# Attention, projection and block transform on one core: x of four projection tiles loaded in the last head, and five output buffers

## The chip, the core and the metric

The kernel runs on one core of a Trainium2 chip. A core has a matrix engine (TensorE, "PE" in the profile, its weight loads "PEld"), VectorE ("DVE"), ScalarE ("ACT"), GpSimd ("POOL"), the synchronisation engine ("SP"), which in this kernel only issues transfers, and 16 DMA engines that all queues share. The on-chip memory is called SBUF, the memory of the matrix results PSUM. The metric is the device time of one execution in microseconds; less is better. A time is the median of several runs. The profile is of one further execution.

## The reference

x has the shape (1, 48, 256, 256) in float32. Two layers follow each other, each with a group normalisation and a residual:

```python
x = x + L0(gn(x))     # attention over 4x4 patches, 8 heads
x = x + L1(gn(x))     # three matrices over w, h and c in 64x64 windows
```

```python
def L0(x, w_qkv, w_dw, temperature, w_proj):
    qkv = jnp.einsum('bchw,oc->bohw', x, w_qkv)
    qkv = dwconv3x3(qkv, w_dw)
    q, k, v = heads(unfold(split(qkv)))          # 8 heads, 96 x 4096 (and a border)
    q, k = l2norm(q), l2norm(k)
    attn = softmax(einsum('bhcn,bhcm->bhnm', q, k) * temperature)
    out = fold(einsum('bhcn,bhnm->bhcm', v, attn))
    return einsum('bchw,oc->bohw', out, w_proj)

def L1(x, Ws, Hs, Cs):
    xb = x.reshape(B, C, H // 64, 64, W // 64, 64)
    return einsum('bcphqw,twW,thH,tcC->bCpHqW', xb, Ws, Hs, Cs).reshape(B, C, H, W)
```

The functions are shortened; "..." of shapes and padding is left out.

## The kernel before, in words

**Stages.** First x is read once for its statistics, the pointwise part of two heads is computed and head 0 is convolved (`depthwise_first`). Then the eight heads run, in a block whose instructions keep the order in which they are written (`tc.manual_schedule()`). Then comes the projection with the first residual and the statistics of the second layer (lines 726 to 788), and at last the second layer in 64 x 64 windows (from line 791).

**A head.** A head has 16 groups (`NG`) of two blocks of 128 rows. For each block `scores` (L337, L566) multiplies 128 queries with all 4096 keys and takes exponentials into a tile `e` of 16 KB a partition; there are three such tiles. `weigh` (L595, L606) then multiplies the exponentials of both blocks with the values and adds to four accumulators `oacc`, one for each k of `NK` = 4. While a head runs, the convolution of the next head is done beside it by `Depthwise`, and the next head's keys and values are loaded. In the last head (`more` is false) there is none of that. `load_query(h, g + 2)` is issued on SP in group g, into one of two buffers.

**Keys.** Head h has eight key tiles of 4 KB a partition, `keys[h, m]`, in 14 buffers taken in turn. Tile m of head h is number 8h + m, so the last head's eight tiles fall in places 0 to 7 of the ring.

**Outputs.** In the last group of a head, `store(h, m)` for m = 0 to 7 transposes a piece of the accumulators (L612), copies it from PSUM into `oo` (L614, ScalarE, two buffers of 2 KB) and issues two transfers of 96 KB from the POOL queue to the buffer `os_` in device memory (L616). Outputs 0 and 1 come after k = 1, 2 and 3 after k = 2, 4 and 5 after k = 3, 6 and 7 at the end.

**Projection.** It has 8 tiles (t) of 16 rows in each half of the picture; both halves lie side by side in 96 partitions. For each tile and half SP loads `pot` (the outputs, L740) and `pxt` (x, L741), 48 x 16 KB = 768 KB each, into pools of three buffers. Tile 0 needs outputs 0 and 4, tiles 2t and 2t+1 need outputs t and t+4. TensorE projects in four steps (L746), VectorE adds x in place (L753) and takes statistics (L757), and POOL issues the store of the sum (L762) to `x1s`. The x load of tile t + 3 goes into the buffer that tile t's store reads. This part has no written order: it is ordered at build time by readiness and by place in the program. Each engine then carries out its own list strictly in order, SP and POOL as queues of transfers.

**Memory.** Pools lie behind one another from the low end of a partition. Before the change, behind the constants: `cv` (the convolution's buffers, 52 KB), `ahead` (queries, 14 key tiles, values), `ae` (three tiles e), `asm` (small tiles and `oo`) and `ao`; the partition is full. A later pool that takes the place of earlier ones waits, with its first instruction, until all tiles of the pools under it have been read for the last time. The pool `pj` (48 KB for pot, 48 KB for pxt) lies over `cv` and `ahead`.

Of the kernel before, what the change touches and what calls it, by code (L numbers as in the profile page):

```python
# [8 lines left out]
F32 = mybir.dt.float32  # L9
F32R = mybir.dt.float32r  # L10
# [6 lines left out]
C = 48  # L17
H = W = 256
HALF = H // 2
P2 = 2 * C  # L20
KS = 4
KK = KS * KS
NH = 8
HD = C * KK // NH
# [9 lines left out]
PX = W // KS  # L34
# [5 lines left out]
TP = 256  # L40
# [5 lines left out]
def conv_preact_kernel(  # L46
# [15 lines left out]
    nc = tc.nc  # L62
    xc = x.rearrange("b c y x -> (b c) y x")
# [34 lines left out]
    for s in range(2):  # L98
        r = slice(s * C, (s + 1) * C)
        for h in range(NH if s == 0 else H0):  # L100
            o = s * M0 + h * HC if h < H0 else (h - H0) * HC
            nc.gpsimd.dma_start(
                out=(wq[r] if h < H0 else wr[0:C])[:, o : o + HC].rearrange("c (z e) -> c z e", z=3),
                in_=w_qkvT.rearrange("c (z h e) -> h c z e", z=3, h=NH)[h],
# [198 lines left out]
    NM = NT // 512  # L303
# [99 lines left out]
    with tc.tile_pool(name="xn", bufs=1) as xnp, tc.tile_pool(name="cst", bufs=1) as cst, tc.tile_pool(  # L403
        name="nps", bufs=2, space=PSUM
# [9 lines left out]
        for i, LR in enumerate(parts):  # L414
            j = sum(parts[:i])
            for s in range(2):
                eng = nc.sync if s == 0 else nc.scalar
                eng.dma_start(
                    out=xr[s * C : (s + 1) * C, j : j + LR, :], in_=xc[:, s * HALF + j : s * HALF + j + LR, :]
# [8 lines left out]
        for g, (w, k) in enumerate(((wq, P2), (wr, C))):  # L428
            m = w.shape[1]
# [48 lines left out]
                nc.sync.dma_start(out=rows, in_=ot[s * M0 : (s + 1) * M0])  # L478

    attention = ExitStack()  # L480
    cv = attention.enter_context(tc.tile_pool(name="cv", bufs=1))
    one = attention.enter_context(tc.tile_pool(name="one", bufs=2, space=PSUM))

    ots = [cv.tile([M1, 4, W + 2], F32, name=f"ot{i}") for i in range(NOT)]
# [5 lines left out]
    with tc.If(nc.values_load(large) > 0):  # L490
# [8 lines left out]
        with tc.tile_pool(name="mk", bufs=NM) as mk, tc.tile_pool(name="mq", bufs=2) as mq, tc.tile_pool(  # L499
            name="mps", bufs=2, space=PSUM  # L500
        ) as mps:
            for h in range(NH):
                kts = []
                for m in range(NM):
                    kt = mk.tile([128, 2, 512], F32R, name="mkt")
# [18 lines left out]
    with tc.tile_pool(name="ahead", bufs=2) as ah, tc.tile_pool(name="ae", bufs=3) as ae, tc.tile_pool(  # L524
        name="asm", bufs=6
    ) as asm, tc.tile_pool(name="ao", bufs=1) as ao, tc.tile_pool(name="big", bufs=3, space=PSUM) as big:
        MB = 8
        NK = NB // MB
        NG = NB // G
        keys, queries, values, oaccs = {}, {}, {}, {}  # L530

        def load_key(h, m, eng=nc.sync):
            keys[h, m] = ah.tile([128, 2, 512], F32R, name="kt", bufs=14)
            load_keys(keys[h, m], h, m, eng)

        def load_query(h, g):
# [71 lines left out]
        def store(h, m):  # L608

            pt = one.tile([HD, 4, 128], F32, name="pt", tag="one")  # L610
            for i in range(4):
                nc.tensor.transpose(pt[:, i, :], oaccs[h, m // 2][:, m % 2, i * HD : (i + 1) * HD], ident)  # L612
            oo = asm.tile([HD, 512], F32, name="oo", bufs=2)
            nc.scalar.copy(oo, pt.rearrange("p i n -> p (i n)"))  # L614
            for i in range(512 // TP):
                nc.gpsimd.dma_start(  # L616
                    out=os_[m * (512 // TP) + i, h * HD : (h + 1) * HD, :], in_=oo[:, i * TP : (i + 1) * TP]
                )
# [16 lines left out]
        with tc.manual_schedule():  # L635
            load_query(0, 1)
            block = scores(0, 0)
            for h in range(NH):
                more = h + 1 < NH
                rows = {r: Depthwise(h + 1, r) for r in range(CR + 1)} if more else {}  # L640
                for g in range(NG):
                    p, d, n = rows.get(g - 2), rows.get(g - 1), rows.get(g)

                    if h == 0 and 0 < g <= 6:
                        load_value(0, g + 1)
                    if more and CR + 2 <= g < CR + 6:
                        for m in range(2):
                            load_value(h + 1, (g - CR - 2) * 2 + m)
                    if more and CR + 3 <= g < CR + 6:
                        for m in range(2):  # L650
                            load_key(h + 1, (g - CR - 3) * 2 + m)

                    blocks = [normalised(*block)]
                    if p:
                        p.norm()
                        p.root()
                    block = scores(h, g * G + 1)
                    if more and g == NG - 1:
                        load_key(h + 1, 6)
                        load_key(h + 1, 7, nc.gpsimd)  # L660
                    if g + 2 < NG:
                        load_query(h, g + 2)
                    elif more:
                        load_query(h + 1, g + 2 - NG)
                    if p:
                        p.scale()
                    if d:
                        for t in range(1, 4):
                            d.tap(t)
                    second = block  # L670
                    if g + 1 < NG:
                        block = scores(h, (g + 1) * G)
                    elif more:
                        block = scores(h + 1, 0)
                    blocks.append(normalised(*second))
                    if d:
                        for t in range(4, 9):
                            d.tap(t)

                    if g == 0 and rows:  # L680
                        rows[0].load()

                    if h == 0 and 0 < g <= 6:
                        turn(0, g + 1)
                    if more and CR + 2 <= g < CR + 6:
                        for m in range(2):
                            turn(h + 1, (g - CR - 2) * 2 + m)
                    if g == 0 and h > 0:
                        for m in range(6, 8):
                            store(h - 1, m)  # L690
                    if p:
                        p.patches()
                        p.store((2,))
                        p.high()
                    if d:
                        d.square()
                    if n:
                        n.first()
                    for k in range(NK):
                        s = (h * NG + g) * NK + k  # L700
                        weigh(h, g, blocks, k)
                        if k == 0 and d:
                            d.reduce()
                        if k == 0 and p:
                            p.low(nc.gpsimd)
                            p.store((0, 1))
                        if s % 2:
                            for w in strips[s - 1] + strips[s]:
                                w.run(big.tile([128, 2, 512], F32, name="big"))
                            for w in strips[s + 1] + strips[s + 2]:  # L710
                                w.load()
                        elif s:
                            for w in strips[s - 2] + strips[s - 1]:
                                w.store()
                        if k == 2 and g + 1 in rows:
                            rows[g + 1].load()

                        if g == NG - 1 and k > 0:
                            for m in range(2 * k - 2, 2 * k):
                                store(h, m)  # L720
            for m in range(6, 8):
                store(NH - 1, m)
# [1 line left out]


    l1c = ctx.enter_context(tc.tile_pool(name="l1c", bufs=1))
    RP = TP // PX * KS
    NP = TP
    with tc.tile_pool(name="pj", bufs=3) as pj, tc.tile_pool(name="pjs", bufs=1) as pjs, tc.tile_pool(
        name="pps", bufs=3, space=PSUM  # L730
# [2 lines left out]
        ov = os_.rearrange("t (c k) n -> t c k n", k=KK)  # L733
        for t in range(HALF // RP):
            ot = pj.tile([P2, KK, NP], F32, name="pot")
            xt = pj.tile([P2, RP, W], F32, name="pxt")
            for s in range(2):
                r = slice(s * C, (s + 1) * C)
                y0 = s * HALF + t * RP
                nc.sync.dma_start(out=ot[r], in_=ov[s * (NT // 2 // TP) + t])  # L740
                nc.sync.dma_start(out=xt[r], in_=xc[:, y0 : y0 + RP, :])  # L741
            xv = xt.rearrange("p (py ki) (px kj) -> p ki kj py px", ki=KS, kj=KS)
            for ki in range(KS):
                ps = pps.tile([P2, KS, NP], F32, name="pps")
                for i in range(0, KS, 2):
                    nc.tensor.matmul(  # L746
                        ps[:, i : i + 2, :],
                        lhsT=wp,
                        rhs=ot[:, ki * KS + i : ki * KS + i + 2, :],
                        start=True,  # L750
                        stop=True,
                    )
                nc.vector.tensor_add(  # L753
                    xv[:, ki], ps.rearrange("p k (py px) -> p k py px", py=RP // KS), xv[:, ki]
                )
            for i in range(0, RP, 2):
                nc.vector.bn_stats(  # L757
                    st1[:, (t * RP + i) // 2, :], xt[:, i : i + 2, :].rearrange("p a b -> p (a b)")
                )
            for s in range(2):  # L760
                y0 = s * HALF + t * RP
                nc.gpsimd.dma_start(out=x1s[:, y0 : y0 + RP, :], in_=xt[s * C : (s + 1) * C])  # L762
# [23 lines left out]
        nc.tensor.matmul(pb1, lhsT=mrow, rhs=csn[0:C], start=True, stop=True)  # L786
        cbias = l1c.tile([128, T3 * C], F32, name="cbias")
        nc.vector.tensor_copy(cbias, pb1)


    with tc.tile_pool(name="lx", bufs=3) as lx, tc.tile_pool(name="lz", bufs=2) as lz, tc.tile_pool(
# [173 lines left out]
```

## Time and profile before

| what | us |
|---|---|
| time, median of 3 runs (3700.89 to 3706.79) | 3703.03 |
| the profiled execution | 3698.24 |
| its span, to which the profile's shares refer | 3696.2 |
| last head, first scores to last weighing | 2849 to 3222.85 |
| last output store issued | 3238.5 |
| first x load and first output load of the projection issued | 3210.05 and 3221.21 |
| first and last matmul group of the projection | 3238.89 and 3362.70 |
| last statistics of the projection done | 3379.9 |
| first load of the second layer issued | 3384.66 |

| engine | busy us | share of the span |
|---|---|---|
| PE | 3466.8 | 94% |
| PEld | 2905.8 | 79% |
| DVE | 2139.4 | 58% |
| ACT | 1873.3 | 51% |
| POOL | 542.9 | 15% |

How to read the profile: times are us from the span's start. "L746" is line 746 of the kernel. A group is written as line, engine, operation, output <- input. "Idle before" tells how long an engine had stood still and what ended that. The granted clock is the share of its full clock that TensorE was given. The DMA share is the mean busy share of the 16 DMA engines. The chain of waits goes back from the last instruction: at each step to what released it.

### The profile page before, as it was taken

Reading aid. Unit: us, or ns where it says so; the run is one execution under the profiler, and the core shown is the slowest. Engines: PE = TensorE matmul, PEld = TensorE weight load, DVE = VectorE, ACT = ScalarE, POOL = GpSimd, SP = SyncE. Lnnn points to the kernel's source line nnn. Section 1 sums busy time; section 2 is a strip of 40 time slices with the busy share of each in tenths; the row PEclk is TensorE's granted clock in tenths of the full one; section 3 lists DMA queues with packets and bytes.
Section 4 is the critical chain, followed back from the end, with each engine's and each line's share of the span. In section 5 each row is a group of like instructions: output and inputs, shape, how many; then the busy total and the mean of one; then the engine's idle time right before and its main releaser. Section 6 shows DMA issues by size and latency. Waiting matters only on the chain.

```text
span 3696.2 us, 100318 instructions
## 1 busy us (share of the span) xinstructions
PE 3466.8 (94%) x44252; PEld 2905.8 (79%) x44252; DVE 2139.4 (58%) x3514; ACT 1873.3 (51%) x2747; POOL 542.9 (15%) x628
## 2 busy tenths in 40 slices
PE   2869999999999999999999999999999999855998
PEld 1337777898888898988888989888889888713776
DVE  5454774189628953894399349925982222266654
ACT  0235676566546654665566556655664444300332
POOL 2030111012111211121122112201220000000011
PEclk9989999999999999999999999999999999966999
DMA  7455666533323332333233323332333100299774
GB/s 160 152 133 153 176 170 171 149 96 95 94 79 82 93 89 75 83 90 96 73 92 86 87 73 93 86 87 84 94 79 87 36 19 19 51 248 197 127 138 92
DMA packets 274146, 386.48 MB, mean 105 GB/s; under 512 B 77010, under 2 KB 211522, under 8 KB 269480
## 3 DMA queue, kind: packets, MB, share of 16 engines
q1 hardware_dynamic: 234790, 264.95, 27.4%
q0 software_dynamic: 35424, 106.40, 12.4%
q10 hardware_dynamic: 3490, 8.64, 1.1%
q8 instruction: 350, 5.73, 0.7%
q14 instruction: 92, 0.75, 0.1%
HBM read 234.76 MB, written 144.90 MB: 103 GB/s over the span
## 4 chain that ended last, share of the span: by engine, by line
PE 82%; DMA 6%; DVE 2%; issue 1%; SPq 1%; ACT 1%; ACTq 0%; POOL 0%; POOLq 0%; DVEq 0%
PE big L337 36%; PE big L595 35%; PE pb L863 4%; PE pa L841 2%; PE pc L880 2%; DMA pxt<-in_x_dram 2%; DMA t<-ot 1%; PE big L177 1%; DVE acc L228 1%; PE pt L612 1%; DMA pad<-t 1%; PE pn L247 1%; DMA pot<-os__70 1%; PE pst L549 1%; DMA x1s<-pxt 0%
## 5 line engine op out<-in xcount | busy, mean ns | idle before, releaser
L566 ACT ACTIVATE e<-big,nmx 128x1024 f32<-128x1024 f32 x1024 | 1143.8, 1118 | 875.5 <-PE big L337 613.1
L337 PE MATMUL big<-kt,qt 128*128 128x512 f32 x6144 | 1436.7, 392 | 31.1 <-DMA kt<-qkv 29.0
L595 PEld LDWEIGHTS big<-vn,e 128*64 128x64 f32 x32768 | 1357.0, 137 | 57.2 <-ACT e L566 30.6
L595 PE MATMUL big<-vn,e 128*64 128x96 f32 x32768 | 1387.3, 247 | 6.1 <-DVE oacc L606 2.5
L337 PEld LDWEIGHTS big<-kt,qt 128*128 128x128 f32 x6144 | 1144.6, 188 | 279.6 <-issue 28.8
L606 DVE TENSOR_TENSOR oacc<-big,oacc 128x768 f32<-128x768 f32 x480 | 453.4, 954 | 713.0 <-PE big L595 713.0
L228 DVE SCALAR_TENSOR_TENSOR acc<-pad,dwt,acc 126x1024 f32<-126x1024 f32 x592 | 765.5, 1293 | 39.8 <-ACT acc L209 24.0
L295 POOL DMA_DIRECT2D qkv<-o x72 | 52.8, 734 | 1240.7 <-ACT o L279 1240.7
L579 DVE TENSOR_REDUCE zt<-zs 128x1 f32<-128x4 f32 x256 | 38.4, 150 | 335.1 <-ACT e L566 335.1
L289 POOL TENSOR_TENSOR ol<-o,oh 126x1024 fp32r<-126x1024 f32 x78 | 184.9, 2370 | 311.1 <-DVE ss L243 237.8
L566 ACT ACTIVATION_READ_ACCUMULATOR e<-big,nmx 128x1 f32 x1024 | 196.3, 192 | 0.0
L848 DVE TENSOR_TENSOR lzt<-pa,cbias 128x864 f32<-128x864 f32 (+1 forms) x88 | 137.0, 1628 | 96.4 <-PE pa L841 96.4
L870 ACT COPY lyt<-pb 128x512 f32<-128x512 f32 x144 | 84.5, 587 | 212.4 <-PE pb L863 212.4
L279 ACT COPY o<-acc 126x1024 f32<-126x1024 f32 x74 | 159.1, 2150 | 0.0
L863 PEld LDWEIGHTS pb<-wsb,lzt 128*64 128x64 f32 x2304 | 126.1, 138 | 27.6 <-issue 19.5
L616 POOL DMA_DIRECT2D os__70<-oo x128 | 65.2, 515 | 541.6 <-ACT oo L614 541.3
L863 PE MATMUL pb<-wsb,lzt 128*64 128x128 f32 x2304 | 142.0, 279 | 1.3 <-issue 1.3
L746 PE MATMUL pps<-pot,wp 96*96 96x512 f32 x128 | 79.1, 787 | 61.5 <-DMA pot<-os__70 61.5
L239 ACT ACTIVATE sq<-acc 126x1024 f32<-126x1024 f32 x74 | 78.2, 1057 | 100.7 <-DVE acc L228 100.7
L180 ACT ACTIVATE ot<-big,bias 108x1024 f32<-108x1024 f32 x64 | 68.2, 1111 | 113.1 <-PE big L177 71.4
L209 ACT ACTIVATE acc<-pad,dwt 126x1024 f32<-126x1024 f32 x74 | 84.1, 1137 | 80.6 <-DMA pad<-t 80.6
L746 PEld LDWEIGHTS pps<-pot,wp 96*96 96x96 f32 x128 | 26.9, 219 | 113.3 <-issue 79.0
(124 smaller groups left out, 1977.0 us busy)
## 6 DMA issues: line engine op xcount, KB each, us to landing
pad<-t SPq DMA_DIRECT2D x238, 254.0 KB
t<-ot SPq DMA_DIRECT2D x128, 217.7 KB
qkv<-ol POOLq DMA_DIRECT2D x78, 336.0 KB, 6.1
qkv<-oh POOLq DMA_DIRECT2D x70, 336.0 KB, 5.6
qt<-qkv SPq DMA_DIRECT2D x176, 96.0 KB
xs<-in_x_dram SPq DMA_DIRECT2D x128, 96.0 KB
os__70<-oo POOLq DMA_DIRECT2D x128, 96.0 KB, 2.1
pxt<-in_x_dram SPq DMA_DIRECT2D x16, 768.0 KB
```

Source lines behind the costliest of these rows:

```text
L209: nc.scalar.mul(self.acc, self.pad[:, 0:KS, 0:W], dwt[:, self.h, 0:1])
L228: nc.vector.scalar_tensor_tensor(self.acc, self.pad[:, dy : dy + KS, dx : dx + W], dwt[:, self.h, tap : tap + 1], self.acc, ALU.mult, ALU.add,
L279: nc.scalar.copy(self.o.rearrange("p (a b) x -> p a b x", a=KS), self.acc.rearrange("p a (x b) -> p a b x", b=KS))
L289: eng.tensor_sub(self.ol, self.o, self.oh.bitcast(F32))
L337: nc.tensor.matmul(ps[:, i, :], lhsT=qt[:, r, q0 : q0 + 128], rhs=kts[2 * j + i][:, r // 2, :], start=(r == 0), stop=(r == 2),)
L566: nc.scalar.activation(e[:, j * 1024 : (j + 1) * 1024], ps.rearrange("p a b -> p (a b)"), AF.Exp, bias=nmx[:, b : b + 1], accum_out=zs[:, ...
L595: nc.tensor.matmul(ps[p : p + 64, j // 4, j % 4 * HD : (j % 4 + 1) * HD], lhsT=e[:, mb * 128 + p : mb * 128 + p + 64], rhs=vn, start=(i == 0),
L606: nc.vector.tensor_add(oaccs[h, k], ps[:, :, : 4 * HD], oaccs[h, k])
L746: nc.tensor.matmul(ps[:, i : i + 2, :], lhsT=wp, rhs=ot[:, ki * KS + i : ki * KS + i + 2, :], start=True, stop=True,)
L848: nc.vector.tensor_tensor(zv[:, :, y0 : y0 + n, :], pa[:, :, : n * T3 * C].rearrange("p s (y k) -> p s y k", y=n), cbias.rearrange("p (u v ...
L863: nc.tensor.matmul(pb[s * WS : (s + 1) * WS, i, :], lhsT=zts[u][:, t * C + c + i, :], rhs=wsb[:, t, :], start=True, stop=True,)
L870: nc.scalar.copy(yt[:, t, :], pb.rearrange("p i x -> p (i x)"))
```

## The change

The convolution's pool `cv` is opened at the other end of the partition, and a second pool there, `kb`, takes key places 8 to 13; places 0 to 7 stay in `ahead`. At the first group of the last head both are closed, and a pool `pe` opens in their place. It holds four tiles of x (`xts`, 16 KB each) and five buffers for the last five outputs (2 KB each). In groups 1 to 8 of the last head, after the weighing steps k = 1 and k = 3, SP issues a quarter of a tile of x for both halves: 192 KB each, 32 in all. The projection takes x of tiles 0 to 3 from there and loads only that of tiles 4 to 7. The pool is closed after the projection. The sum of the memory stays the same.

```diff
-    cv = attention.enter_context(tc.tile_pool(name="cv", bufs=1))
+    convolution = ExitStack()
+    cv = convolution.enter_context(tc.tile_pool(name="cv", bufs=1, side="right"))
+    kb = convolution.enter_context(tc.tile_pool(name="kb", bufs=6, side="right"))
+    NX = 4
...
+        NLATE = 5
+        RP = TP // PX * KS
...
         def load_key(h, m, eng=nc.sync):
-            keys[h, m] = ah.tile([128, 2, 512], F32R, name="kt", bufs=14)
+
+            first = (h * NM + m) % 14 < 8
+            keys[h, m] = (ah if first else kb).tile([128, 2, 512], F32R, name="kt", bufs=8 if first else 6)
             load_keys(keys[h, m], h, m, eng)
...
-            oo = asm.tile([HD, 512], F32, name="oo", bufs=2)
+            late = h == NH - 1 and m >= NM - NLATE
+            oo = (pe if late else asm).tile([HD, 512], F32, name="oo", bufs=NLATE if late else 2)
...
+                    if not more and g == 0:
+                        convolution.close()
+                        early = ExitStack()
+                        pe = early.enter_context(tc.tile_pool(name="pe", bufs=1, side="right"))
+                        xts = [pe.tile([P2, RP, W], F32, name=f"xt{t}") for t in range(NX)]
...
+                        if not more and 0 < g <= 2 * NX and k in (1, 3):
+                            i = (g - 1) * 2 + k // 2
+                            t, y = i // 4, i % 4 * (RP // 4)
+                            for half in range(2):
+                                y0 = half * HALF + t * RP + y
+                                nc.sync.dma_start(
+                                    out=xts[t][half * C : (half + 1) * C, y : y + RP // 4, :],
+                                    in_=xc[:, y0 : y0 + RP // 4, :],
+                                )
...
-            xt = pj.tile([P2, RP, W], F32, name="pxt")
+            xt = xts[t] if t < NX else pj.tile([P2, RP, W], F32, name="pxt")
             for s in range(2):
                 r = slice(s * C, (s + 1) * C)
                 y0 = s * HALF + t * RP
                 nc.sync.dma_start(out=ot[r], in_=ov[s * (NT // 2 // TP) + t])
-                nc.sync.dma_start(out=xt[r], in_=xc[:, y0 : y0 + RP, :])
+                if t >= NX:
+                    nc.sync.dma_start(out=xt[r], in_=xc[:, y0 : y0 + RP, :])
...
+    early.close()
```

More of the change, by code (lines that the diff above doesn't have):

```diff
@@ L726, in conv_preact_kernel @@
     l1c = ctx.enter_context(tc.tile_pool(name="l1c", bufs=1))
-    RP = TP // PX * KS
     NP = TP
```

## The prediction

> **What bounds the kernel now.** I read the page's slices first, to find the stage that the change touches.
>
> ```profile
> PE   2869999999999999999999999999999999855998
> PEclk9989999999999999999999999999999999966999
> DMA  7455666533323332333233323332333100299774
> ```
>
> A slice is 3696.2 / 40 = 92.4 us. TensorE is full from the third slice to the 34th: that is the attention, and there only matrix work counts. In slices 32 to 34 (the last head) the DMA row falls to 1, 0, 0: nothing is left to prepare. In slices 36 and 37 TensorE falls to 5 and its clock to 6 while DMA stands at 9. That is the projection. A table by stage gives the sizes; its columns are the stretch, its length, busy time (and instructions) of PE, PEld, DVE, ACT, POOL, then granted clock, DMA share, GB/s.
>
> ```profile
> 2654.00:2742.00 88.00, 88.00 (x1225) 78.88 (x1224) 80.75 (x137) 59.29 (x81) 20.17 (x16) 1.00 0.34 85
> 2896.00:3199.00 303.00, 303.00 (x4203) 270.97 (x4200) 72.37 (x167) 135.03 (x224) 0.00 (x0) 1.00 0.07 19
> 3210.00:3233.00 23.00, 15.80 (x284) 14.35 (x284) 4.26 (x7) 3.20 (x6) 6.08 (x12) 0.91 0.70 151
> 3233.00:3362.00 129.00, 69.06 (x112) 23.52 (x112) 87.22 (x84) 2.45 (x3) 9.11 (x18) 0.70 1.01 255
> ```
>
> The last row is the projection's body: DMA share 1.01, the busiest engine (VectorE) at 87 of 129 us. It is bound by transfers: 129 us x 255 GB/s = 32.9 MB, which is 41.8 transfers of 48 x 16 KB = 0.786 MB, so **3.09 us for one transfer**. The row before it is the seam between head and projection, where the queue is 0.70 full. The chain of waits shows why:
>
> ```profile
> 3217.24 4.19 DMA os__70<-oo
> ...
> 3222.91 6.54 DMA os__70<-oo
> ...
> 3230.93 2.07 DMA os__70<-oo
> 3233.00 0.18 SPq L740
> ...
> 3235.43 32.32 DMA pxt<-in_x_dram
> ```
>
> The output stores of the last head go through two buffers, so each of three rounds waits for the landing of the round before (4.19 and 6.54 us; the third, alone, needs 2.07, the others share the rings with the two x loads issued at 3210.05). SP then waits at the second half of the first output load (L740), which reads what output 4 stored. In the waits of the SP queue from 3210 to 3390 the largest that repeats is for stores of the projection, before a new x load may overwrite a buffer:
>
> ```profile
> SPq L741 <- DMA x1s<-pxt: 81.2, 5, 22.4
> SPq L740 <- DMA os__70<-oo: 21.5, 3, 10.9
> ```
>
> **Part 1, the five output buffers.** In the timeline the last weighing ends at 3222.85 and the transposes of outputs 4 and 5 run at 3222.78 to 3223.86, but the copy of output 4 comes at 3229.55. With a buffer of its own it follows its transpose. The price is read at the end of the head before, where the rings were quiet: weighing ended at 2873.13, output 4's store was issued at 2874.66, 1.5 us later. So here 3222.85 + 1.5 = 3224.4, landing after another 2.07: 3226.4 instead of 3233.0, **6.6 us earlier**. Output 2 still shares two buffers with 0 and 1; its copy could start at 3219.6, output 0's store (issued 3216.73) lands at 3219.2, so this wait costs nothing. If that cover goes (a late landing), output 2 delays 4 on ScalarE and up to the 6.6 us are lost.
>
> **Part 2, where the projection's buffers lie.** Before, the first load waited until the values were last read (SP: 42.2 us on L585, until 3210.05). After it, with the convolution pool and six key buffers moved to the other side, the pool "pj" lies over the exponentials "e", whose last reader ends at 3222.85. The first load of outputs then starts at 3222.9 instead of 3221.2. Its cover is the wait for output 4 (3226.4): nothing, and 1.7 us without it.
>
> **Part 3, the x loads that go.** Sixteen x loads become eight. Two of the eight removed (tile 0) ran at 3210 to 3221 in the seam and cost the body nothing; six stood in the body: 6 x 3.09 = **18.5 us**. Against this, two more output stores now fall into the loaded stretch: about 0.39 MB, 0.39 / 255 GB/s = 1.5 us. A second sum, by VectorE: the first matmuls of tiles 0 and 4 stand at 3238.9 and 3308.2, 69.3 us apart; a tile costs VectorE 7.63 us for four additions and 4.88 for eight statistics (tile 2's rows), 12.5, with its waits on TensorE some 12.8. Four tiles in 51.2 give 18.1. The two agree because 2 loads and 2 stores a tile (4 x 3.09 = 12.4) are as long as VectorE's work. A load's price is bounded by 255 GB/s in the mixed body and by 209 GB/s for x loads alone at the kernel's start (3.76 us): 18.5 to 22.6. I take the mixed row, which is this stage.
>
> **Part 4, the x pieces that are added.** In groups 1 to 8 of the last head SP issues 32 pieces of 0.197 MB, four a group, behind the six query loads. The timeline issues a queue load in some 0.43 us, so 1.7 us of SP a group; SP waited 250.7 us in 14 waits for TensorE there, 17.9 each, so the slots are empty. On the rings a group's four pieces are 0.786 MB, 3.1 us (3.8 at 209 GB/s) in a group of 11.10 + 10.71 = 21.8 us whose share is 0.07. The next query is issued a whole group later and is needed 21.8 us after that. Does the traffic slow TensorE? At 85 GB/s in head 6 the weighing took 10.71 us, at 19 GB/s in head 7 also 10.71. Cost nothing, covered by TensorE's 303 of 303 us; were each group to lose what its pieces take on the rings it would be 8 x 3.1 = 25 us. The first piece must find the convolution and the head-6 keys released: those keys were last read before 2849, the piece comes after 2880.
>
> The Trainium skill speaks against part 4: "DMA: Bandwidth & Descriptors" says under "Bandwidth" to batch to 1 MiB, and under "Anatomy of one DMA" gives 2 us a transfer beside the bytes at 436 GB/s. By it, as an estimate, 32 pieces cost 78 us of latency where the eight whole loads cost 30, and a removed load is worth 1.8 us in a full queue, 16 us in all here. The body's 3.09 contradicts its byte rate, and the trace of before has no piece in that place.
>
> **Part 5, pools moved at the start.** Keys keep their rotation: eight buffers and six, met in the old order of fourteen, so every reuse is as far away as before. The convolution's first writes wait for the statistics' pool today (POOL, until 138.81) and will again, since the far side also overlaps it: 0, bounded by a scheduling shift of some 3 us either way, the copies and landings of that stage.
>
> **Sum.** 6.6 + 18.5 - 1.5 = 23.6. The profiled execution took 3698.24 (span 3696.2), the median of three is 3703.03, 0.13% above; the same stretch goes from either. Span 3672.6, median 3703.0 - 23.6 = **3679**.
>
> **Rivals.**
>
> *VectorE becomes the bound* (0.13). If SP runs ahead and x of tiles 4 to 6, whose three buffers are free at once, comes in early, the last tile doesn't wait for a load. Additions could start at 3242.8 - 6.6 = 3236.2; eight tiles at 12.5 and 2 us for the first one's matmuls end at 3338 where the statistics now end at 3379.9: 42 us, 3661. For it: the rings moved 301 GB/s in the stretch 3260 to 3272. Against it: at 255 GB/s some 36 transfers still need 111 us from 3226.4, and the last tile took 17.3 us (3362.6 to 3379.9) behind its last load, which is 3355.
>
> *The pace stays, only the seam is gained* (0.17). SP works in order: x of tile 4 waits behind the outputs of tile 3, these for TensorE's tile 0, later x for stores that land 13.2 us (median) after issue. If this loop and not the traffic sets the 18 us a tile, only the 6.6 us come: 3696; half of part 3 gives 3687. For it: the 81.2 us of waits above. Against it: with DMA at 1.01 those waits are the full queue itself.
>
> *Queries come late in the last head, and it is slower* (0.08). One SP queue carries pieces and queries. A piece that waits for its region or a completion holds the next group's query; its slack is 21.8 us less some 5 for issue and landing, about 17. Beyond that every us is lost by TensorE, up to eight times. It decides from 23.6 / 8 = 3 us a group beyond the slack, a hold of 20; at 24 us held it would be 8 x 7 - 23.6 = 32 slower, 3735. Against it: releases lie 30 us back, and nothing else uses the rings.
>
> **How the numbers follow.** Forecast 0.62. From no change this kernel's measurement can tell about 0.2%, 7.4 us. Within it falls a part of the second rival, 0.05; the rest of it, the forecast and the first make faster 0.87; slower 0.08. The range starts at 3664, most of the first rival, and ends at 3692, where half of the second is in: 0.8 inside.
>
> **What would show it.** Store of output 4 near 3224 and no wait of ScalarE for stores after output 2: part 1. First projection matmul near 3232 instead of 3238.9. Tiles 0 to 3 some 13 us apart, 4 to 7 some 18, DMA at 1.0 from 3226: part 3. The last weighing still at 3222.85, weighing 10.71, no TensorE wait for queries: part 4. If the head ends late, part 4 is wrong; if tiles 0 to 3 keep 18 us with idle rings, the order of the queue decides and not the traffic; if 4 to 7 also run at 13, VectorE does.

## The result, and the profile after

The changed kernel takes **3698.52 us** (median of 20 runs, 3687.25 to 3709.12), the kernel before 3702.22 beside it (20 runs, 3692.88 to 3711.41): ratio 0.9989, 95% interval 0.998 to 0.9999. That is less than 0.2%, so no change that this kernel's measurement tells from none, where 23.6 us were forecast. The profiled execution took 3698.42, with a span of 3696.5 (before: 3698.24 and 3696.2).

The slices of the page of the changed kernel, the same rows as before:

```profile
PE   2869999999999999999999999999999999965998
PEclk9989999999999999999999999999999999975999
DMA  7465665533323332333233323332333221099674
```

The new transfers of the last head show (2, 2, 1 where 1, 0, 0 stood), and the weak spot in slices 36 and 37 is a little smaller. Nothing in these rows tells why the gain is missing. The table by stage (the stretch, its length, busy time of PE, PEld, DVE, ACT and POOL, granted clock, DMA share, GB/s) shows the last head and the projection:

```profile
2896.00:3199.00 303.00, 303.00 (x4251) 271.52 (x4251) 73.28 (x168) 133.02 (x221) 2.02 (x4) 1.00 0.17 42
3233.00:3362.00 129.00, 83.14 (x272) 32.89 (x273) 91.53 (x90) 5.09 (x9) 15.16 (x30) 0.74 0.95 244
```

TensorE stays full while the pieces of x come in. So the span was cut at points that both traces have: the first score matmul of heads 0, 1, 2 and 7 and the first load of the second layer, in us. (Head 7 of the kernel before begins at 2854.5 by this count; the matmuls at 2849 are still the last block of head 6.)

| kernel | start to head 0 | head 0 | head 1 | heads 2 to 6 | head 7 to the load | load to the end |
|---|---|---|---|---|---|---|
| before | 272.7 | 429.4 | 361.8 | 1790.5 | 530.2 | 311.5 |
| after | 269.5 | 429.3 | 366.5 | 1804.3 | 508.5 | 318.5 |

The part that the change is about gained 21.7 us. **Heads 1 to 6 lost 18.4** (from unrounded times). The rest can't be told from chance in one profile of each: the first column lies between 269.3 and 277.6 over all kernels of this study, and the last between 311.4 and 313.8 in every kernel but this one profiled execution.

The loss lies in the score matmuls. The chain of waits in head 2, first of the kernel before, then of the changed one (start, duration, what):

```profile
1128.34 10.96 PE big L337 x48
...
1150.37 10.96 PE big L337 x48
```

```profile
1130.40 11.08 PE big L337 x48
1141.48 10.71 PE big L604 x256
1152.56 11.08 PE big L337 x48
```

The weighing takes 10.71 us as before. The scores take 0.12 us more for 48 matmuls, with no wait between the pieces and the granted clock at 1.00 in both. All instructions of the score line, before and then after (least, median and greatest duration in ns, first and last start):

```profile
L337 PE MATMUL big<-kt,qt x6144: 387/389/767, 272.7 to 3207.3; 128*128 128x512 f32 x199
```

```profile
L337 PE MATMUL big<-kt,qt x6144: 387/393/768, 269.5 to 3222.4; 128*128 128x512 f32 x199
```

How much a head loses depends on how many of its eight key tiles lie in the new pool `kb`. The times of GpSimd's key loads, one set a head, show it:

| from one head's loads to the next | key tiles of the head in `kb` | before | after | more |
|---|---|---|---|---|
| head 1 | 6 | 361.84 | 366.42 | 4.58 |
| head 2 | 2 | 358.07 | 360.35 | 2.28 |
| head 3 | 4 | 358.07 | 361.14 | 3.07 |
| head 4 | 4 | 358.08 | 361.19 | 3.11 |
| head 5 | 2 | 358.07 | 359.68 | 1.61 |
| head 6 | 6 | 358.23 | 361.89 | 3.66 |

That is 18.31 us over 24 tiles, 0.76 a tile and head. A tile is met by 32 blocks of queries with three matmuls each, 96 matmuls: 7.9 ns each. The starts of neighbouring score matmuls in the trace (heads 1 to 6, tiles 2 to 6 of each) lie 226.9 ns apart before; after, 233.3 on tiles in `kb`, 227.9 on others, and 231.5 on a tile of `ahead` that follows one of `kb`. So 6.4 of the 7.9 ns fall on the tiles in `kb` themselves, the rest on the tiles beside them.

### The profile page after: what moved, and what is told of

The parts are those of the page before. It is cut to its first block, busy times and chain, and to the rows that moved or that the text cites. A ratio compares the mean times of both kernels' runs of the same rounds, so it can differ in the third digit from the quotient of the medians.

```text
span 3696.5 us, 100340 instructions
## 1 busy us (share of the span) xinstructions
PE 3486.2 (94%) x44252; PEld 2909.4 (79%) x44252; DVE 2134.8 (58%) x3514; ACT 1872.2 (51%) x2747; POOL 541.8 (15%) x628
## 4 chain that ended last, share of the span: by engine, by line
PE 84%; DMA 4%; DVE 2%; issue 1%; ACT 1%; SPq 1%; POOL 0%; ACTq 0%; POOLq 0%; DVEq 0%
PE big L337 37%; PE big L604 36%; PE pb L888 4%; PE pa L866 2%; PE pc L905 2%; DMA pxt<-in_x_dram 1%; PE big L177 1%; DVE acc L228 1%; PE pt L621 1%; DMA pad<-t 1%; PE pn L247 1%; PE pst L558 1%; DMA vt<-qkv 0%; DMA kt<-qkv 0%; DMA lxq<-x1s 0%
## 5 line engine op out<-in xcount | busy, mean ns | idle before, releaser
L337 PE MATMUL big<-kt,qt 128*128 128x512 f32 x6144 | 1452.8, 395 | 31.1 <-DMA qt<-qkv 21.5
L243 DVE TENSOR_REDUCE ss<-sq 126x64 f32<-126x1024 f32 x80 | 97.5, 1219 | 23.3 <-ACT sq L239 23.3
```

What stands on the lines that cost most here:

```text
L243: nc.vector.tensor_reduce(self.ss, self.sq.rearrange("p a (x b) -> p x a b", b=KS), AX.XY, ALU.add)
L337: nc.tensor.matmul(ps[:, i, :], lhsT=qt[:, r, q0 : q0 + 128], rhs=kts[2 * j + i][:, r // 2, :], start=(r == 0), stop=(r == 2),)
```

## The experiments

**1. Only the layout.** Theory: where the keys lie slows the scores. Rival: the new transfers or the output buffers do it. The edit is shown against the changed kernel.

```diff
-    NX = 4
+    NX = 0
...
-            late = h == NH - 1 and m >= NM - NLATE
-            oo = (pe if late else asm).tile([HD, 512], F32, name="oo", bufs=NLATE if late else 2)
+            oo = asm.tile([HD, 512], F32, name="oo", bufs=2)
...
                         convolution.close()
-                        early = ExitStack()
-                        pe = early.enter_context(tc.tile_pool(name="pe", bufs=1, side="right"))
-                        xts = [pe.tile([P2, RP, W], F32, name=f"xt{t}") for t in range(NX)]
...
-                        if not more and 0 < g <= 2 * NX and k in (1, 3):
...
-            xt = xts[t] if t < NX else pj.tile([P2, RP, W], F32, name="pxt")
+            xt = pj.tile([P2, RP, W], F32, name="pxt")
...
-    early.close()
```

> Only the moved memory is left of the change: convolution and six key buffers at the far end, keys in two pools; x and the outputs go as before. Theory (the six key buffers lie badly for TensorE): heads 1 to 6 lose what they lose in the changed kernel, some 18 us between the key loads of POOL at 695 and 2866, a score matmul on the moved keys paced 234 ns instead of 227; median some 15 us above before (3715 to 3722). Rival (x pieces or the late buffers slow the heads, by a changed order): heads 1 to 6 as before, median within 4 us of before.

Measured 3728.07 us, ratio 1.0068 (1.0053 to 1.0084). Heads 1 to 6 take 365.9 and 1803.7, as in the changed kernel; 233.3 and 227.9 ns are found again. So the layout alone causes the loss in the heads. There is a second one, and with it the median lies 6 us above the range that was expected: from head 7 to the load it takes 540.1 instead of 530.2. The timeline of SP shows it:

```profile
3242.92 0.30 SPq L749 DMA_DIRECT2D pot<-os__70  x1
3243.27 0.42 SPq L751 DMA_DIRECT2D pxt<-in_x_dram  x1
```

The last weighing began at 3228.24 and ended at 3242.8. The projection's pool now lies over `e`, so x of tile 0 waits for that end; before, it was issued at 3210.05, as the last weighing began. In the changed kernel x of tile 0 is there already, and only the first output load waits for that end.

**2. The changed kernel, and 32 bytes.** The addresses in a partition (bytes, from the built program) gave an idea: queries begin at 21216, the lower keys at 27360, the upper ones at 151808. The lower ones are 6144 = 24 x 256 from the queries. The upper ones are not a multiple of 128 away. An unused tile of 32 bytes in `cv`, the pool that lies above `kb`, moves them down to 151776, which is 510 x 256 from the queries.

```diff
     ots = [cv.tile([M1, 4, W + 2], F32, name=f"ot{i}") for i in range(NOT)]
+    gap = cv.tile([128, 8], F32, name="gap")
+    nc.gpsimd.memset(gap, 0.0)
     for t in ots:
```

> The changed kernel with an unused piece of 32 bytes added to the convolution's pool, so that the six moved key buffers begin at 151776 instead of 151808 bytes: the same remainder by 64 (and by 512) as the queries' buffers, as all keys and queries of the kernel before had among themselves. Theory of the phase (a weight load and the moving rows meet badly when their addresses differ in phase): pace back to 227 ns, heads 1 to 6 lose nothing, median some 18 us below the changed kernel, about 3680. Rivals of the place (a high address, or far from the queries): pace 234 ns, time as the changed kernel, 3698.

Measured **3677.34 us, ratio 0.9927 (0.9907 to 0.9948)**. All score matmuls start 226.8 ns apart; heads 1 to 6 take 361.8 and 1790.0, head 7 to the load 508.2. So it is neither two pools nor a high address as such.

**3 and 4. High addresses with equal remainders.** In the changed kernel `kb` is opened ahead of `cv`, so that its tiles begin at 204768; and in the kernel before the pool `ahead` goes to the other end (queries 147936, keys 154080).

```diff
+    kb = convolution.enter_context(tc.tile_pool(name="kb", bufs=6, side="right"))
     cv = convolution.enter_context(tc.tile_pool(name="cv", bufs=1, side="right"))
-    kb = convolution.enter_context(tc.tile_pool(name="kb", bufs=6, side="right"))
```

```diff
-    with tc.tile_pool(name="ahead", bufs=2) as ah, tc.tile_pool(name="ae", bufs=3) as ae, tc.tile_pool(
+    with tc.tile_pool(name="ahead", bufs=2, side="right") as ah, tc.tile_pool(name="ae", bufs=3) as ae, tc.tile_pool(
```

> The changed kernel with the six key buffers at the very top (from 204768) and the convolution below them (from 151808). Their remainder by 64 is then 32, that of the queries. Theory of the phase: 227 ns, heads 1 to 6 lose nothing. Theory of a high address: 234 ns or worse, the loss of 18 us stays. Theory of the convolution's neighbourhood: between these.

> The kernel before with its pool of queries, all 14 keys and values at the high end (queries from 147936, keys 154080 to 211424), the phase between queries and keys unchanged. Theory of a high address: all keys slow, 234 ns in every head, some 5 us a head, 40 us in all. Theories of the phase and of the distance between queries and keys: 227 ns, time as before.

One run each: 3678.14 and 3715.97 us. Both have 226.7 to 226.8 ns on all keys. The first is a second way to the full gain. The second has its 13 us more from head 7 to the load (543.2); its projection pool too lies over `e`, as in experiment 1.

**5. The kernel before, spoilt by 32 bytes.** If the relation of the two operands decides, 32 bytes between queries and keys must slow a kernel that has one pool and no other part of the change. The keys go to 80352, with the queries at 74176.

```diff
         load_query(0, 0)
+        gap = ah.tile([128, 8], F32, name="gap", bufs=1)
+        nc.gpsimd.memset(gap, 0.0)
```

> The kernel before with one unused piece of 32 bytes between its query and its key buffers: nothing moves to another pool, only the remainder by 64 of all 14 keys (32) differs from that of the queries (0). Theory of the phase: every score matmul is paced some 234 ns instead of 227, 768 a head, so 5.4 us a head and 43 us in eight; median about 3740 to 3748. Rival (two pools, or the far place of the six buffers, were slow, and 32 bytes cured it by chance): 3702, heads of 358.1 us as before.

Measured 3737.88 us, ratio 1.0097 (1.0073 to 1.0121): 38 us slower, 363.2 a head where 358.7 stood (mean of heads 1 to 6). The chain of waits in head 2 of this kernel:

```profile
1119.03 11.40 PE big L337 x48
1141.50 11.25 PE big L337 x48
1163.82 11.25 PE big L337 x48
```

Every key is slow here, 233.4 to 233.5 ns, and so are the blocks: 11.25 us instead of 10.96, and 11.40 where the kernel before has 11.13. A head loses 4.5 us where 5.4 had been expected. The keys' own remainder by 256 is now 224, the same as in the fast kernel of experiment 2; what differs is the remainder of the queries, 192 here and 224 there. So **the relation decides, not the place of the keys**.

**6 and 9. By what number the remainders must agree.** The unused tile is made 96 and 160 bytes long. Then the upper keys agree with the queries by 64 but not by 128, and by 128 but not by 256.

```diff
-    gap = cv.tile([128, 8], F32, name="gap")
+    gap = cv.tile([128, 24], F32, name="gap")
```

```diff
-    gap = cv.tile([128, 8], F32, name="gap")
+    gap = cv.tile([128, 40], F32, name="gap")
```

> The changed kernel with 96 bytes instead of 32: keys from 151712, remainder 32 by 64 (the queries': 32), but 32 by 128 (the queries': 96). If 64 bytes is the period: 227 ns, heads of 358.0 us, as with 32 bytes. If the period is 128 or more: 234 ns on the moved keys and the loss of 18 us back.

> The kernel after with an unused tile of 160 bytes at the head of the pool of the convolution, so that the upper key tiles begin at byte 151648: equal to the queries' 21216 by 32, 64 and 128, different by 256 (96 against 224). The 160 bytes are written once at the start. If the period of the slower pace is 128 bytes, the score matmuls on the upper key tiles start 227 ns apart as on the lower ones, heads 2 to 6 last 358.0 to 358.1 us each, and the span is that with a gap of 32 bytes, 3676 to 3684. If it is 256 bytes, they start 233 to 234 ns apart, the heads last 359.5 to 362 us, and the span is 3692 to 3700.

One run each: 3698.59 us (span 3696.6) and 3698.51 us (span 3696.5). Both have the slow pace on the upper keys. All runs together, with the distance from the queries to the keys modulo 256 and the mean distance of starts:

| kernel | lower keys: remainder, ns | upper keys: remainder, ns |
|---|---|---|
| before | 0, 226.9 | 0, 226.9 |
| after | 0, 227.9 | 32, 233.3 |
| 1 layout alone | 0, 227.9 | 32, 233.3 |
| 2 gap of 32 | 0, 226.8 | 0, 226.8 |
| 3 `kb` on top | 0, 226.7 | 0, 226.8 |
| 4 `ahead` high | 0, 226.7 | 0, 226.7 |
| 5 before, gap of 32 | 32, 233.4 | 32, 233.5 |
| 6 gap of 96 | 0, 228.2 | 192, 233.3 |
| 9 gap of 160 | 0, 227.4 | 128, 232.7 |

A remainder of 0 by 256 goes with the fast pace in each row, each other that was tried (32, 128 and 192) with the slow one. The lower keys at 227.4 to 228.2 are those of kernels whose upper keys are slow. It need not be 512: in experiment 3 the distance is 717 x 256, an odd multiple. How the pace arises inside the chip was not tried.

**7, 10 and 11. The output buffers.** The kernel with the 32 bytes, and the same one whose last five outputs use the two rotating buffers. The pair was run twice; the second time both on one chip.

```diff
-            late = h == NH - 1 and m >= NM - NLATE
+            late = False
```

> The changed kernel with the 32 bytes, without the five output buffers (all outputs through the two old ones). Theory (the output rounds were slow because the x loads of tile 0 shared the rings, and these are gone): from the first score matmul of the last head to the first load of the second layer some 508 to 512 us as with both, median 3677 to 3682. Rival (the two buffers are a wait of their own): some 6 us more, 514, median 3684.

> The kernel after with the 32 bytes, as in the run of that name, timed beside the one with the x loads alone. Both theories: 3674 to 3682 us, with 508 us from the first score matmul of head 7 to the next layer's first load.

> The kernel after with the 32 bytes and the early x loads, but the last five outputs of a layer in the two buffers that rotate. If the five buffers save what the prediction gave them (6.6 us), it is 5 to 8 us slower than the kernel with both, 3681 to 3688 us, and its stretch from the first score matmul of head 7 to the next layer's first load is 514 to 516 us, as in the one profile there is. If what was seen in that profile was chance, the two are within 2 us of each other.

Without the buffers: 3678.94 us (4 runs, ratio 0.9939, 0.9916 to 0.9962) where the kernel with them had 3677.34 on another chip. In the second pair 3684.68 (0.9947, 0.9934 to 0.9961) against 3676.50 (0.9923, 0.991 to 0.9936): 8 us, and the intervals overlap by only 0.0002. The profiles don't give one answer. From head 7 to the load they show 514.9 against 508.2 in the first pair and 505.6 against 506.4 in the second. There the two profiled executions are 9.8 us apart, of which 6.0 lie in head 0 (440.5 against 434.5), which the edit doesn't touch. What two buffers can do is seen in the chain of the first one:

```profile
3232.88 8.49 DMA os__70<-oo
...
3242.85 15.48 DMA os__70<-oo
3258.35 0.04 ACTq L626
3258.39 0.04 issue
3258.43 0.59 ACT oo L626
```

An output waited 15.48 us for the landing of one before it, among loads of SP: four of 768 KB go out from 3241.56 to 3243.7. In the second pair's profile (11) the longest such landing on the chain is 6.60. So the buffers take away a wait that was long in one of the two profiles. What they are worth in the median, between 0 and 8 us, stays open.

**8. Outputs alone.** The kernel with the 32 bytes, and no early x.

```diff
-    NX = 4
+    NX = 0
```

> The changed kernel with the 32 bytes and the five output buffers, but all sixteen x loads in the projection. Theory (the gain is the x loads'): from the first score matmul of the last head to the second layer some 533 to 540 us, more than before (530), since the projection's buffers now lie over the exponentials and x of tile 0 can't come under the last weighing; median 3703 to 3712. Rival (the gain is the outputs'): below 520, median under 3690.

Measured 3711.64 us, ratio 1.0028 (1.0013 to 1.0043). Heads 1 to 6 are fast (361.8 and 1790.0), but head 7 to the load takes 539.4, 31 us more than with early x. The gain is that of the x loads, and without them the pool over `e` costs 9 us.

## Why the prediction was wrong, point by point

**Part 5 is the step that failed**: "Keys keep their rotation: eight buffers and six, met in the old order of fourteen, so every reuse is as far away as before", priced 0 and bounded by 3 us. The order of reuse did hold: the chain shows no new wait in the heads. But moving tiles changed their addresses, and with these the pace of 24 tiles' matmuls in heads 1 to 6: +18.3 us. Experiments 2 and 3 take the loss away by the addresses alone, 5 makes it in the kernel before with 32 bytes, and 6 and 9 narrow down which distances do it. The trace of before could not show it, for there all operands agree. What could have been bounded is the number of instructions that the step touches: 6144 score matmuls of 227 ns are on the path, and with the 3% that is known now this is 42 us. Experiment 5 pays 38.

**Part 3, the x loads, was right and too small.** Additions of tile 0 to tile 7 were 123.7 us apart (3242.78 to 3366.44) and are now 102.0 (3257.80 to 3359.80): 21.7 us instead of 18.5, inside the bounds of 18.5 to 22.6; shared over the six loads, 3.6 us each. The first additions of tiles 0 to 4 lie 50.8 us apart; the second sum by VectorE had said 51.2. The largest waits of the SP queue in this stretch show the rest, of the changed kernel:

```profile
SPq L763 <- DMA os__70<-oo: 61.0, 2, 53.0
SPq L763 <- PE pps L770: 48.6, 5, 12.2
...
SPq L765 <- DMA x1s<-pxt: 19.5, 1, 19.5
```

The waits for the projection's stores fell from 81.2 us (5) to 19.5 (1); SP now waits for TensorE to free the outputs' buffers. The rival by which the order of the queue keeps the old pace is out, and so is the one by which VectorE's 12.5 us hold to the end: the last three tiles are 14.3, 20.5 and 16.4 apart.

**Part 1, the seam, came and was eaten.** The chain of the changed kernel:

```profile
3224.94 6.99 PE big L604 x124
...
3239.53 0.59 PE pt L621 x4
...
3240.14 0.59 ACT oo L624
...
3241.02 6.82 DMA os__70<-oo
...
3247.86 5.92 DMA pot<-os__70
...
3253.91 6.38 PE pps L770 x8
```

Output 4 is copied right behind its transpose, and its store goes out 1.5 us after the weighing's end instead of 7.6: 6.1 of the 6.6 us. Then two things take it back. From the issue on the landing takes 6.82 us, 4.3 more than before (3230.43 to 3233.00, 2.57), where 2.07 had been put in. The rings were not quiet: SP issued the first output load of the projection (768 KB) at 3239.62, just ahead of the store at 3241.02, while before it was issued at 3221.21. The stretch of this landing, before and then after (columns as in the table by stage):

```profile
3230.40:3233.00 2.60, 1.73 (x8) 1.24 (x7) 0.00 (x0) 0.22 (x1) 2.03 (x4) 0.50 0.38 110
```

```profile
3241.00:3247.80 6.80, 0.90 (x8) 0.55 (x6) 0.00 (x0) 2.56 (x4) 4.04 (x8) 0.85 0.91 177
```

The other kernels show the same by the number of loads issued just ahead of this store: with one, 6.46 to 6.85 us (2, 10, 11 and the changed kernel; in 11 only the stores of outputs 4 and 5 go along), with two, 11.97 and 12.36 (8 and 1).

And the first 124 matmuls of the last weighing take 6.99 us instead of 5.34, at a granted clock of 0.76 instead of 1.00; this is not the change's doing, for in experiments 6 and 9, which have the whole change, they take 5.34, and the first addition comes 31.2 and 31.3 us after the start of the last weighing instead of 32.9. From the start of the last weighing to the first projection matmul it is 28.97 us, as before (3209.92 to 3238.89, 3224.94 to 3253.91). The error in the prediction's sum was to take a landing from quiet rings into a stretch that the change itself fills.

**Part 2, the pool over `e`**: the first output load went out at 3239.62, at the weighing's end, as the prediction had it, and SP waits for output 4 behind it in any case. But "nothing" was not its price: issued there, it is the load beside which the landing of output 4 takes 6.82 us. The 1.7 us without that cover stand in no run. Where x of tile 0 is loaded in the projection too, the pool over `e` costs 9 to 10 us (experiments 8 and 1). In 8 the first addition comes 38.2 us after the start of the last weighing instead of 32.9, and from there to the load of the second layer it takes 145.7 instead of 141.9.

**Part 4, the pieces**: nothing, as forecast. TensorE is busy 303.00 of 303 us with a DMA share of 0.17 where 0.07 stood, and the weighing keeps 10.71. The rival of late queries did not occur: the first score matmul of head 7 and the start of its last weighing lie 355.4 us apart before and after. The first piece was issued at 2920.5; head 6's keys had been read until head 7 began, at 2869.5. The pieces of 192 KB under a busy engine cost nothing here. As for the removed loads, the Trainium skill's figures that were weighed there ("DMA: Bandwidth & Descriptors", "Anatomy of one DMA"; the page gives them for transfers issued from GpSimd, these are SP's) make 6 x 1.8 = 10.8 us of them, an estimate, and 16 us of the whole change; the 78 us given there for the pieces are 64 of fixed time and 14 of bytes. The measured 21.7 us for the six stand further from 10.8 than from the 18.5 of the mixed row.

**The sum after the fact**: 18.3 lost in the heads, 21.7 gained from head 7 on, 3.4 us together; the medians differ by 3.7, closer than executions that spread over 20 us can confirm. With the 32 bytes the loss goes, and the medians of two series are 25.1 and 28.5 us below the kernel before (the profiles show 22.0 and 23.8 of it from head 7 on); 23.6 had been forecast. That the gain stands so near the forecast is in part luck: the seam gave nothing where 6.6 us had been counted, and the body of the projection 21.7 where 18.5 - 1.5 stood.

## What to carry to other kernels

Where a change moves tiles, write down the addresses of both operands of the matmul that fills the path, and for matmuls like these keep their distance a multiple of 256 bytes; an unused tile of a few bytes does it. A step priced at nothing because no wait changes still needs a bound by the number of instructions that it touches: one nanosecond on 6144 matmuls is 6 us. And a duration measured on quiet rings holds only as long as the change leaves them quiet, while a pool laid over tiles that are read last holds back the first load into it, here to the moment when the last stores need the rings.

## What the runs showed of the hardware that was not expected

**The distance between a matmul's operands.** A score matmul of 128 x 128 with 128 x 512 (declared float32r in the kernel, f32 in the profile) starts every 226.7 to 226.9 ns where all moving operands lie a multiple of 256 bytes from the stationary one, and every 232.7 to 233.5 ns at distances that leave 32, 128 or 192: 3%. The Trainium skill ("TensorE: Matmul & The Clock Gate", "Part 2: What happens when you issue a matmul") says that loading the next weights does not take read bandwidth from the running matmul, since both have a port of their own. Experiment 5 shows that here the pace depends on the two addresses together; that the reads meet somewhere is a guess that no run here tests.

**The granted clock after a short pause.** The first part of the last weighing, after the same idle 1.87 us, before and then after (columns as in the table by stage):

```profile
3209.90:3215.20 5.30, 5.28 (x125) 5.17 (x125) 1.39 (x4) 0.00 (x0) 0.00 (x0) 1.00 0.90 167
```

```profile
3224.90:3231.90 7.00, 6.96 (x125) 6.84 (x125) 0.96 (x1) 0.00 (x0) 0.00 (x0) 0.76 0.06 10
```

In nine of the thirteen profiles these first 124 matmuls take 6.95 to 6.99 us, in four (before, 5, 6 and 9) 5.34. The transfers under them don't decide it: before and 5 have a DMA share of 0.90 and 0.88 there, but 6 keeps a clock of 1.00 with almost none:

```profile
3234.20:3239.50 5.30, 5.24 (x124) 5.15 (x124) 0.96 (x2) 0.00 (x0) 0.00 (x0) 1.00 0.09 14
```

Experiment 6 is the kernel of experiment 2 with a longer unused tile, and 2 has 0.75 there. In the changed kernel the trace has the clock at half for 3.41 us (3225.25 to 3228.66). What decides whether this follows the pause was not tried.
